# An attention and mixture-of-experts layer on one core: first sequence packed in quarters, slots cleared in pieces, first scatters at half pace, and later expert tiles two deep

## The chip, the cores and the metric

The kernel runs on one core of one Trainium2 chip. A core has TensorE (PE in the profile; its weight loads are listed as PEld), VectorE (DVE), ScalarE (ACT), GpSimd (POOL) and SyncE (SP). SP only issues transfers here. The metric is the device time in microseconds (us). The times shown are medians; one execution was also recorded by the hardware profiler.

## The reference

Eight sequences of 512 tokens with 128 features go through one layer: causal attention with 16 heads of 8 features, then a mixture of 8 experts of which each token uses two.

```python
# x: (8, 512, 128)
x = x + attn(layernorm(x))
#   s = (q * scale) @ k.T per head, causal mask, softmax, p @ v, then @ Wo + bo
x = x + ffn(layernorm(x))
#   probs = softmax(x_flat @ gate_w.T); topk_probs, topk_idx = top_k(probs, 2)
#   hidden = relu(einsum('th,ehf->tef', x_flat, w1) + b1)      # f = 512
#   all_out = einsum('tef,efh->teh', hidden, w2) + b2
#   y = sum over the two chosen experts of all_out * topk_probs
```

The kernel computes an expert only for the tokens that chose it.

## The kernel before

**Lanes.** The program is written by seven generators, called lanes here: `setup` (L175), `project` (L265), `shifts` (L355), `attend` (L450), `route` (L582) with `dispatch` (L675) inside it, `experts` (L756) and `sums` (L886). Each of them yields a due time, counted in sequences: 3.5 is halfway through the attention of sequence 3. The main loop at the end of the kernel always lets the lane with the smallest due time write its next instructions. The order in which instructions are written is the order on PE, ACT, DVE and SP. So the due times alone set what stands before what on each engine. POOL's indirect transfers are put in order with its masking instructions by `in_order` (L438).

**Attention.** `project` loads a sequence (L98), normalizes it, makes q and k, splits each into bf16 parts and writes the parts to DRAM (`to_dram`, L300). It reads them back packed by heads (L328) into `q2_buf[b % 2]` and `k2_buf[b % 2]`. For sequence 0 the q transfers go through SP's queue and the k transfers through ACT's; from sequence 1 on, all go through SP's. `shifts` computes the scores once (S, L393), takes the row maxima on DVE (L416), transposes them (`nmT`, L364) and writes them as two more rows into the packed q (L370). `attend` computes the scores again, transposed and with the maxima included (ST, L549), then the exponential on ACT (L555), the causal selection on POOL (L561) and the product with the values (L479). S runs 0.55 of a sequence ahead of ST.

**Experts.** The sequences form three groups: 0 to 3, 4 to 6, and 7. When the last sequence of a group is routed, `dispatch` gives each token two slots, sorted by expert in tiles of 128, and writes its rows there with indirect transfers (L734, two per 128 tokens; 32, 24 and 8 of them). The slots of a group, `xs`, were cleared before that by `setup` (L227), because a tile has empty places. The groups have 39, 31 and 15 tiles, 85 in all. `experts` works through them. Four tiles (a quad) are loaded at a time (`gather`, L807) and transposed on PE (L832, copied by ACT at L834). Per tile, SP loads the weights of the tile's expert (`wt`, 258 KB, L765), PE computes `ph` (L854, 8 instructions), ACT in even tiles (L862) or DVE in odd ones (L864) adds the bias and takes the relu into `hT`, PE computes `py` (L783, L788) one tile later, and DVE copies it into `yo` (L792). A quad is stored with one transfer (L797). `ph`, `py` and the transposes share three PSUM buffers (`ps_mm`); the attention scores have four (`ps_sc`).

**Sums.** `sums` fetches the two result rows of each token with indirect transfers (L917, one per 128 tokens and choice, 64 in all), and DVE multiplies them by their gate values and adds them to x (L899). Ten buffers hold the rows. A finished sequence is stored (L892).

The start and pace of each group's tiles are given by hand:

```python
    TILES_AT = ((5.56, 0.0705), (8.35, 0.03), (9.29, 0.03))
```

Of the kernel before, what the change touches and what calls it, by code (L numbers as in the profile page):

```python
# [18 lines left out]
P = 128  # L19
# [5 lines left out]
def preln_attn_moe(ctx: ExitStack, tc: tile.TileContext, x, wq, wk, wv, wo, bo,  # L25
# [149 lines left out]
    def setup():  # L175
# [34 lines left out]
        for l in range(3):  # L210
# [3 lines left out]
            if l < 2:  # L214
                rest = const.tile([E, D], F32, tag=f"b2r{l}", name=f"b2r{l}")
                V.tensor_tensor(rest, left, part, ALU.subtract)
                left = rest
        for e in range(E):
            yield 0.6 + 0.3 * e
            nc.sync.dma_start(out=wrows[e, :, 0:F], in_=w1[e])  # L220
            nc.sync.dma_start(
                out=w2_sb.rearrange("p (c e h) -> p c e h", c=FC, e=E)[:, :, e],
                in_=w2[e].rearrange("(c p) h -> p c h", p=P),
            )
        for k in range(len(GROUPS)):
            yield 3.1 + 0.3 * k
            nc.sync.dma_start(  # L227
                out=xs[k].rearrange("(c p) d -> p c d", p=P),
                in_=zeros.unsqueeze(1).to_broadcast([P, xs[k].shape[0] // P, D]),
            )  # L230
# [34 lines left out]
    def project():  # L265
        for b in range(B):
# [31 lines left out]
            def to_dram(s, dst, slots):  # L298
                for c, slot in slots:
                    queue[s].dma_start(  # L300
                        out=dst[slot].rearrange("d h t -> h d t"), in_=part[s][:, c, :]
# [11 lines left out]
            to_dram(0, q_parts, ((0, 0), (0, 3), (1, 1), (1, 4)))  # L313
            yield b - 1.18
            to_dram(0, q_parts, ((2, 2),))
            to_dram(1, k_parts, ((0, 0), (1, 1), (2, 2)))
# [6 lines left out]
            q2, k2 = q2_buf[b % 2], k2_buf[b % 2]  # L323
            for n in (slice(0, HG), slice(HG, H)) if b == 0 else (slice(0, H),):
                for s, dst, src in ((0, q2, q_parts), (1, k2, k_parts)):
                    for r in range(3):
                        o = r if src is q_parts else 0
                        queue[s].dma_start(  # L328
                            out=dst[24 * r : 24 * r + 24, n],
                            in_=src[o : o + 3, :, n].rearrange("c d h t -> (c d) h t"),  # L330
                        )
# [23 lines left out]
    def shifts():  # L355
# [11 lines left out]
        def rows(b, g, nmT):  # L367

            for l in range(2):
                nc.sync.dma_start(  # L370
# [304 lines left out]
    def dispatch(k, soon):  # L675
# [55 lines left out]
        for i in range(n * NT):  # L731
            yield soon(0.037 if group[-1] == B - 1 else 0.044)
# [23 lines left out]
    def experts():  # L756
        tiles = [(k, i) for k, g in enumerate(GROUPS) for i in range(tiles_of(len(g)))]
        wt, yo, at = {}, {}, {}

        def fetch(n):  # L760
            if n < len(tiles):
                k, i = tiles[n]
# [123 lines left out]
    def sums():  # L886
# [19 lines left out]
        t = 0  # L906
# [70 lines left out]
```

## Time and profile before

| | us |
|---|---|
| median of 9 runs | 784.3 (775.51 to 789.34) |
| profiled execution | 785.02 |
| its span | 783.3 |
| first scores (S) start | 31.24 |
| ST of sequence 0, 3, 5, 6 starts | 48.0, 216.5, 339.4, 417.4 |
| scatters of group 0 | 317.7 to 366.8 |
| first and eighth tile of group 0, ninth | 390.0, 425.4, 437.3 |
| attention ends | 568.0 |
| scatters of group 1 end | 584.1 |
| first tile of group 1, of group 2 | 601.0, 710.1 |
| last `py` ends | 765.2 |

The times of the profile count from the start of the span. Each row of a table of stretches gives a start and an end, the length, then the busy time of PE, PEld, DVE, ACT and POOL with the number of instructions in brackets, the mean clock that the throttle granted to TensorE as a share of full speed, the busy share of the DMA engines, and GB/s. In a row of the timeline stand the start, the duration, the engine, the line of the kernel, the operation and its tiles; in square brackets the time for which the engine was idle before it, and what ended that. "remote" is a release whose origin the profile doesn't tell. A row of waits gives the engine, operation and line that waited, what it waited for, the total in us, how often, and the longest.

### The profile page before, as it was taken

How to read it: one execution, taken by the hardware profiler on the slowest of the kernel's cores; microseconds unless marked ns; L12 is line 12 of the kernel's file. 1: busy time of each engine (PE TensorE's matmuls, PEld its weight loads, DVE VectorE, ACT ScalarE, POOL GpSimd, SP SyncE). 2: the span in 40 equal slices, each digit the busy share in tenths (PEclk: the TensorE clock that was granted, in tenths of full speed). 3: DMA queues.
4: the chain of work that ended last, by engine and by line, in shares of the span. 5: the costliest groups of instructions: out<-in, count | busy, mean ns of one | idle time of the engine just before them, and what ended most of it. 6: DMA issues, size and time to landing. Idle time of an engine off the chain costs nothing. (4 is left out here: it accounts for less than half of the span.)

```text
span 783.3 us, 13582 instructions
## 1 busy us (share of the span) xinstructions
PE 641.6 (82%) x4439; PEld 408.1 (52%) x4439; DVE 434.6 (55%) x1308; ACT 299.3 (38%) x651; POOL 272.2 (35%) x450
## 2 busy tenths in 40 slices
PE   5487898998996998887899799999958749787770
PEld 3233453454453454343467566776547738776660
DVE  3365768679676679534765475675114404341332
ACT  2043464564563563533465245454412112221110
POOL 4022233333332332786221112121760352422433
PEclk9677899898996997867899799998978869998885
DMA  3562164173277260252336422321532526664452
GB/s 91 132 150 41 29 162 110 29 176 96 55 190 232 55 130 7 81 140 77 82 96 147 125 60 80 89 78 39 151 90 68 166 68 170 186 175 135 130 149 64
DMA packets 78977, 84.81 MB, mean 108 GB/s; under 512 B 9852, under 2 KB 63660, under 8 KB 77756
## 3 DMA queue, kind: packets, MB, share of 16 engines
q1 hardware_dynamic: 74164, 73.97, 36.4%
q0 software_dynamic: 4096, 8.40, 3.8%
q10 hardware_dynamic: 648, 1.57, 0.8%
q8 instruction: 37, 0.61, 0.3%
q14 instruction: 32, 0.26, 0.1%
HBM read 57.74 MB, written 27.93 MB: 109 GB/s over the span
## 5 line engine op out<-in xcount | busy, mean ns | idle before, releaser
L416 DVE TENSOR_REDUCE pm<-s 128x1 f32<-128x512 f32 (+2 forms) x320 | 207.1, 684 | 118.7 <-PE s L403 111.4
L555 ACT ACTIVATE pt<-st 128x512 f32<-128x512 f32 x320 | 178.5, 598 | 131.2 <-PE st L549 113.1
L561 POOL TENSOR_SCALAR_AFFINE_SELECT pt<-pt 128x256 f32<-128x256 f32 x256 | 102.0, 412 | 304.5 <-ACT pt L555 302.4
L393 PE MATMUL s<-k,q 72*128 72x512 bf16 (+3 forms) x512 | 127.7, 330 | 16.9 <-DMA k<-ones_bf 12.3
L549 PE MATMUL st<-q,k 74*128 74x384 bf16 (+3 forms) x512 | 117.1, 330 | 13.5 <-DMA q<-nmT 4.4
L479 PE MATMUL po<-pt,va 128*9 128x512 f32 (+3 forms) x1024 | 114.2, 475 | 8.4 <-POOL pt L561 4.5
L854 PE MATMUL ph<-xgT,wt 128*128 128x128 f32 x680 | 103.3, 300 | 18.6 <-DMA wt<-wrows 5.7
L788 PE MATMUL py<-w_sb,hT 128*128 x680 | 108.3, 307 | 0.0
L854 PEld LDWEIGHTS ph<-xgT,wt 128*128 128x128 f32 x680 | 92.8, 212 | 27.0 <-issue 13.6
L788 PEld LDWEIGHTS py<-w_sb,hT 128*128 128x128 f32 x680 | 91.4, 209 | 14.7 <-issue 8.5
L917 POOL DMA_INDIRECT y<-ys,slot x64 | 60.7, 949 | 103.2 <-DMA ys<-yo 44.8
L862 ACT ACTIVATE hT<-ph,wt 128x128 f32<-128x128 f32 x172 | 49.3, 368 | 115.8 <-issue 58.0
L393 PEld LDWEIGHTS <-q 72*128 72x128 bf16 x512 | 50.1, 106 | 76.4 <-issue 49.3
L792 DVE COPY yo<-py 128x128 f32<-128x128 f32 x85 | 24.5, 289 | 115.0 <-PE py L788 65.4
L403 PE MATMUL s<-mask_bf,ident_bf 128*128 128x256 bf16 (+1 forms) x320 | 87.6, 274 | 0.0
L734 POOL DMA_INDIRECT xs<-xn_f,slot x64 | 62.3, 973 | 25.0 <-issue 15.7
L549 PEld LDWEIGHTS <-k 74*128 74x128 bf16 x512 | 47.7, 105 | 41.6 <-issue 21.5
L864 DVE TENSOR_SCALAR hT<-ph,wt 128x128 f32<-128x128 f32 x168 | 47.2, 343 | 32.7 <-PE ph L854 18.6
L479 PEld LDWEIGHTS po<-pt,va 128*9 128x9 f32 x1024 | 23.4, 90 | 69.7 <-issue 43.1
L403 PEld LDWEIGHTS <-ident_bf 128*128 128x128 bf16 x320 | 33.9, 106 | 3.7 <-issue 1.4
L834 ACT COPY xgT<-xgTp 128x512 f32<-128x512 f32 (+1 forms) x22 | 12.6, 572 | 55.5 <-PE xgTp L832 40.8
L832 PE MATMUL xgTp<-ident,xg 128*128 128x128 f32 x85 | 15.2, 306 | 19.6 <-DMA xg<-xs 17.6
(124 smaller groups left out, 520.6 us busy)
## 6 DMA issues: line engine op xcount, KB each, us to landing
wt<-wrows SPq DMA_DIRECT2D x85, 258.0 KB
q<-qparts SPq DMA_DIRECT2D x21, 384.0 KB
k<-kparts SPq DMA_DIRECT2D x21, 384.0 KB
qparts<-part SPq DMA_DIRECT2D x40, 128.0 KB
xg<-xs SPq DMA_DIRECT2D x19, 256.0 KB
ys<-yo SPq DMA_DIRECT2D x19, 256.0 KB
kparts<-part SPq DMA_DIRECT2D x21, 128.0 KB
xs<-zeros SPq DMA_DIRECT2D x1, 2496.0 KB
```

The lines of the kernel that those rows point to most:

```text
L393: nc.tensor.matmul(ps[:, at : at + (t + 1) * P], lhsT=q2[:KS, 2 * n + u, ts(t, P)], rhs=k2[:KS, 2 * n + u, : (t + 1) * P], start=(at == 0) ...
L403: nc.tensor.matmul(dst, lhsT=ident_bf, rhs=mask_bf if i > 0 else mask_bf[:, 0, :], start=False, stop=True, skip_group_check=True,)
L416: nc.vector.tensor_reduce(top, src, AX.X, ALU.max)
L479: nc.tensor.matmul(po[32 * h : 32 * h + VC, j * P :], lhsT=va[:, j, HG * g + h, :], rhs=at_cols(pts[pr], unit, u, at, W), start=(first and ...
L549: nc.tensor.matmul(ps[:, at : at + T - j * P], lhsT=k2[: KS + 2, 2 * n + u, ts(j, P)], rhs=q2[: KS + 2, 2 * n + u, j * P :], start=(at == ...
L555: nc.scalar.activation(pt[:, v, :], ps, AF.Exp, scale=SCALE)
L561: selects[0] = nc.gpsimd.affine_select(out=d, in_=d, pattern=[[0, 2], [1, P]], compare_op=ALU.is_ge, fill=0.0, base=0, channel_multiplier=-1,)
L734: ins = nc.gpsimd.indirect_dma_start(out=xs[k], out_offset=bass.IndirectOffsetOnAxis(ap=slot[k][:, j, i : i + 1], axis=0), in_=xn2[b0 + i ...
L788: nc.tensor.matmul(py, lhsT=hT[:, c, :], rhs=w2_sb[:, bass.ds(at[k, i] + c * E * D, D)], start=False, stop=(c == FC - 1),)
L854: nc.tensor.matmul(ph[:, ts(c, P)], lhsT=wt[k, i][:, ts(c, P)], rhs=xgT[:, ts(i - first, P)], start=True, stop=True,)
L862: nc.scalar.activation(hT[:, c, :], ph[:, ts(c, P)], AF.Relu, bias=bias)
L917: ins = nc.gpsimd.indirect_dma_start(out=y, out_offset=None, in_=ys[k], in_offset=bass.IndirectOffsetOnAxis(ap=slot[k][:, j, s * NT + c : ...
```

## The change

- `project`, sequence 0: the parts of q and k are written and read back in quarters of four heads, in the order write quarter 0, write quarter 1, pack quarter 0, write quarter 2, and so on. That makes 20 writes and 12 packs on SP's queue and 12 and 12 on ACT's. Before, 5 and 6 stood on SP's and 3 and 6 on ACT's.
- `shifts`, sequence 0: the rows of maxima are written through ACT's queue.
- `setup`: the loads of the expert weights and the clearing of the slots become 38 transfers of at most 256 KB, one every 0.085 of a sequence from 0.6 on. Before, the three clearings were one transfer each.
- `dispatch`: the scatters of group 0 have due times 0.09 apart instead of 0.044. As `dispatch` runs inside `route`, the routing of sequence 4 comes after them.
- `experts`, group 0: the tiles begin at 6.35 and are 0.05 apart, instead of 5.56 and 0.0705.
- `experts`, groups 1 and 2: `ph` lies in the score buffers (`ps_sc`), `hT` in the buffers of the exponentials, all `hT` and `yo` are made by ACT, `py` runs two tiles late, the weights lie in seven places of the packed q of even sequences and are fetched six tiles ahead, and the rows lie in eight places of the packed k and are loaded two quads ahead.
- `sums`: the fetched rows lie in five places of the packed q of odd sequences, a little less is left pending, and the last sequence is stored in two halves.

```diff
--- before.py
+++ after.py
+        pieces = []
         for e in range(E):
-            yield 0.6 + 0.3 * e
-            nc.sync.dma_start(out=wrows[e, :, 0:F], in_=w1[e])
-            nc.sync.dma_start(
-                out=w2_sb.rearrange("p (c e h) -> p c e h", c=FC, e=E)[:, :, e],
-                in_=w2[e].rearrange("(c p) h -> p c h", p=P),
-            )
+            pieces.append((wrows[e, :, 0:F], w1[e]))
+            pieces.append((
+                w2_sb.rearrange("p (c e h) -> p c e h", c=FC, e=E)[:, :, e],
+                w2[e].rearrange("(c p) h -> p c h", p=P),
+            ))
         for k in range(len(GROUPS)):
-            yield 3.1 + 0.3 * k
-            nc.sync.dma_start(
-                out=xs[k].rearrange("(c p) d -> p c d", p=P),
-                in_=zeros.unsqueeze(1).to_broadcast([P, xs[k].shape[0] // P, D]),
-            )
+            n = xs[k].shape[0] // P
+            for c in range(0, n, 4):
+                m = min(4, n - c)
+                pieces.append((
+                    xs[k].rearrange("(c p) d -> p c d", p=P)[:, c : c + m],
+                    zeros.unsqueeze(1).to_broadcast([P, m, D]),
+                ))
+        for n, (dst, src) in enumerate(pieces):
+            yield 0.6 + 0.085 * n
+            nc.sync.dma_start(out=dst, in_=src)
...
+            def to_dram(s, dst, slots, n=slice(0, H)):
                 for c, slot in slots:
                     queue[s].dma_start(
-                        out=dst[slot].rearrange("d h t -> h d t"), in_=part[s][:, c, :]
+                        out=dst[slot, :, n].rearrange("d h t -> h d t"),
+                        in_=part[s][HD * n.start : HD * n.stop, c, :],
+                    )
+            def pack(s, n):
+                dst, src = ((q2_buf, q_parts), (k2_buf, k_parts))[s]
+                for r in range(3):
+                    o = r if s == 0 else 0
+                    queue[s].dma_start(
+                        out=dst[b % 2][24 * r : 24 * r + 24, n],
+                        in_=src[o : o + 3, :, n].rearrange("c d h t -> (c d) h t"),
                     )
...
-            to_dram(0, q_parts, ((0, 0), (0, 3), (1, 1), (1, 4)))
-            yield b - 1.18
-            to_dram(0, q_parts, ((2, 2),))
-            to_dram(1, k_parts, ((0, 0), (1, 1), (2, 2)))
+            q_slots = ((0, 0), (0, 3), (1, 1), (1, 4), (2, 2))
+            k_slots = ((0, 0), (1, 1), (2, 2))
+            if b > 0:
+                to_dram(0, q_parts, q_slots[:4])
+                yield b - 1.18
+                to_dram(0, q_parts, q_slots[4:])
+                to_dram(1, k_parts, k_slots)
+            else:
+                quarters = [slice(HG * g, HG * g + HG) for g in range(G)]
+                for g in range(G + 1):
+                    if g < G:
+                        to_dram(0, q_parts, q_slots, quarters[g])
+                        to_dram(1, k_parts, k_slots, quarters[g])
+                    if g > 0:
+                        pack(0, quarters[g - 1])
+                        pack(1, quarters[g - 1])
+                yield b - 1.18
...
-            q2, k2 = q2_buf[b % 2], k2_buf[b % 2]
-            for n in (slice(0, HG), slice(HG, H)) if b == 0 else (slice(0, H),):
-                for s, dst, src in ((0, q2, q_parts), (1, k2, k_parts)):
-                    for r in range(3):
-                        o = r if src is q_parts else 0
-                        queue[s].dma_start(
-                            out=dst[24 * r : 24 * r + 24, n],
-                            in_=src[o : o + 3, :, n].rearrange("c d h t -> (c d) h t"),
-                        )
+            if b > 0:
+                pack(0, slice(0, H))
+                pack(1, slice(0, H))
...
-                nc.sync.dma_start(
+                (nc.scalar if b == 0 else nc.sync).dma_start(
...
-            yield soon(0.037 if group[-1] == B - 1 else 0.044)
+            yield soon((0.09, 0.044, 0.037)[k])
...
+        spare_q = q2_buf[0].rearrange("p h t -> p (h t)").bitcast(F32)
+        spare_k = k2_buf[0].rearrange("p h t -> p (h t)").bitcast(F32)
+        WTS, XGS = H * T // 2 // WROW, H * T // 2 // (4 * D)
+        fetched = [0, 0]
+        def ahead(k):
+            return 3 if k == 0 else WTS - 1
+        def behind(k):
+            return 1 if k == 0 else 2
+        def fetch_to(n):
+            while fetched[0] < min(n, len(tiles)):
...
+                if k == 0:
+                    wt[k, i] = work.tile(
+                        [P, WROW], F32, tag="wt", name=f"wt_{k}_{i}", bufs=4
+                    )
+                else:
+                    wt[k, i] = spare_q[:, ts(fetched[1] % WTS, WROW)]
+                    fetched[1] += 1
+                fetched[0] += 1
...
-            nc.vector.tensor_copy(yo[k, first][:, i - first, :], py)
+            if k == 0:
+                nc.vector.tensor_copy(yo[k, first][:, i - first, :], py)
+            else:
+                nc.scalar.copy(yo[k, first][:, i - first, :], py)
...
-            xg = work.tile([P, 4, D], F32, tag="xg", name=f"xg_{k}_{i}")
+            if k == 0:
+                t = work.tile([P, 4, D], F32, tag="xg", name=f"xg_{k}_{i}")
+            else:
+                q = len([a for a in xg if a[0] > 0]) % XGS
+                t = spare_k[:, ts(q, 4 * D)].rearrange("p (a d) -> p a d", a=4)
+            xg[k, i] = t
...
+                follow = quads[q + 1 : q + 2 + (k > 0)]
...
-            ph = mm_tile(f"ph_{k}_{i}")
+            if k == 0:
+                ph = mm_tile(f"ph_{k}_{i}")
+                hT = work.tile([P, FC, P], F32, tag="hT", name=f"hT_{k}_{i}")
+            else:
+                ph = ps_sc.tile([P, T], F32, tag="sc", name=f"ph_{k}_{i}")
+                hT = work.tile([P, 2, T], F32, tag="pt", name=f"hT_{k}_{i}", bufs=6)
+                hT = hT[:, 0, :].rearrange("p (c t) -> p c t", c=FC)
...
-                if n % 2 == 0:
+                if k > 0 or n % 2 == 0:
...
+            ready = late[: max(0, len(late) + 1 - behind(k))]
+            del late[: len(ready)]
+            for part in ready:
+                second(*part)
...
+            fetch_to(n + 1 + ahead(k))
+            if follow:
                 if i == first + (m - 2 if other else 0):
-                    xg = gather(*follow)
+                    for at_quad in follow:
+                        if at_quad not in xg and (other or at_quad[0] == k):
+                            gather(*at_quad)
+                            if other:
+                                break
...
+        YS = 5
+        got = [0]
...
+                _, b, c, n = done.pop(0)
                 nc.sync.dma_start(
-                    out=out[b].rearrange("(c p) d -> p c d", p=P), in_=xt[b]
+                    out=out[b].rearrange("(c p) d -> p c d", p=P)[:, c : c + n],
+                    in_=xt[b][:, c : c + n],
...
+                n = NT // 2 if b == B - 1 else NT
+                if (c + 1) % n == 0 and j == 1:
+                    done.append([0, b, c + 1 - n, n])
...
-                    add_up(4)
+                    add_up(3)
                     for j in range(2):
-                        y = work.tile([P, D], F32, tag="y", name=f"y_{b}_{c}_{j}", bufs=10)
+                        y = q2_buf[1].rearrange("p h t -> p (h t)").bitcast(F32)[:, ts(got[0] % YS, D)]
+                        got[0] += 1
...
-    TILES_AT = ((5.56, 0.0705), (8.35, 0.03), (9.29, 0.03))
+    TILES_AT = ((6.35, 0.05), (8.35, 0.03), (9.29, 0.03))
```

## The prediction

> **What bounds the kernel now.** I read the page's totals and its forty slices first, then the busy times by stretch, then single timelines. Three engine rows and the granted clock:
>
> ```profile
> PE 641.6 (82%) x4439; PEld 408.1 (52%) x4439; DVE 434.6 (55%) x1308; ACT 299.3 (38%) x651; POOL 272.2 (35%) x450
> PE   5487898998996998887899799999958749787770
> POOL 4022233333332332786221112121760352422433
> PEclk9677899898996997867899799998978869998885
> ```
>
> TensorE (PE) is the bound, but its holes (digits 4 to 7) stand in four places: the start, slices 13 and 14, slice 18, and everything from slice 29 on. The stretches:
>
> ```profile
> 240.00:260.00 20.00, 13.53 (x66) 6.53 (x67) 14.23 (x53) 6.87 (x14) 4.62 (x8) 0.66 0.52 159
> 340.00:360.00 20.00, 17.99 (x111) 8.57 (x110) 8.85 (x18) 8.66 (x16) 16.40 (x23) 0.76 0.70 175
> 417.00:568.00 151.00, 141.29 (x1130) 98.92 (x1128) 84.40 (x269) 70.81 (x163) 37.97 (x76) 0.94 0.37 98
> 601.00:762.00 161.00, 122.62 (x824) 109.06 (x825) 58.37 (x225) 32.42 (x104) 61.07 (x64) 0.86 0.51 143
> 620.00:640.00 20.00, 10.69 (x66) 9.54 (x64) 2.92 (x13) 1.95 (x6) 15.33 (x16) 0.80 0.46 129
> ```
>
> After start and length come PE, PE weight load, DVE, ACT, POOL, clock, DMA share and GB/s. While sequences 6 and 7 run with most of group 0's tiles PE works 141 of 151 us: full. From 601 on, with only tiles left, it works 123 of 161, and in 620-640 half the time although DVE and ACT are almost idle. The timeline there tells why:
>
> ```profile
> 628.82 1.06 PE L854 MATMUL ph<-xgT,wt 128*128 128x128 f32 x8
> 631.51 1.14 ACT L862 ACTIVATE hT<-ph,wt 128x128 f32<-128x128 f32 x4 [5.12 <-remote]
> 637.84 0.29 DVE L792 COPY yo<-py 128x128 f32<-128x128 f32 x1 [13.93 <-remote]
> 642.77 1.13 DVE L864 TENSOR_SCALAR hT<-ph,wt 128x128 f32<-128x128 f32 x4 [4.64 <-remote]
> ...
> 660.78 1.06 PE L854 MATMUL ph<-xgT,wt 128*128 128x128 f32 x8
> 661.93 1.14 ACT L862 ACTIVATE hT<-ph,wt 128x128 f32<-128x128 f32 x4 [0.36 <-PE ph L854]
> ```
>
> At 660.78 ACT starts 0.1 us after the matmuls end (661.84). Those of 628.82 end at 629.88, and DVE takes them up at 642.77. The trace's semaphore events put PE's completions in batches at 625.8, 631.4, 637.8 and 642.8, mean distance 5.7 us, just while POOL issues gathers back to back (620.1-640.3). Where POOL pauses, the delay is under 0.05 us. The cause I don't know; that the two go together I use.
>
> The other holes, SP's queue and the first matmul:
>
> ```profile
> 31.24 0.58 PE L393 MATMUL s<-k,q 72*128 72x512 bf16 x1 [12.25 <-DMA k<-ones_bf]
> 42.12 0.25 ACT L364 COPY nmT<-nmTp 32x128 bf16<-32x128 bf16 x1
> 45.49 1.21 SPq L370 DMA_DIRECT2D q<-nmT  x2
> ...
> 220.05 17.84 SPq L98 DMA_DIRECT2D x<-in_L_attn_x_dram  x1
> 237.99 1.29 SPq L370 DMA_DIRECT2D q<-nmT  x2
> ```
>
> The first scores wait 12.25 us for the packs. Row maxima ready at 42.4 are issued at 45.5, behind the q/k writes of sequence 1 (39.31-45.4). And a load stuck for 17.84 us behind the clearing of the slots holds the row maxima of sequence 3.
>
> **The change, part by part.** All terms are against the profiled execution: span 783.3, itself 785.0, 0.7 above the median of 784.3. A minus is a gain.
>
> *Start.* Before, 8 writes and 12 packs; the first q write goes at 12.31, the last at 19.74, and the first q packs, issued at 22.6, need 7.4 us because three 288 KB k packs are ahead of them. After: 32 writes of 32 KB and 24 packs of 96 KB, 32 of these issues on SP, 24 on ACT. At 0.35-0.6 us an issue, 32 take 11-19 us; SP's eleven of before, with their waits, end at 26.1. The first quarter's 8 writes take 4 us from 12.3, land after 2.3 (row: a 128 KB write) at 19, and its 96 KB packs land 2.5-2.9 us after issue when nothing is ahead (row: the first k packs), but stand behind quarter 1's writes. I get 24.5 if nothing collides, and the old 31.2 or later if everything queues; I take 29: -2. ACT holds 24 issues before va and the second sequence's xnT: at 0.4 us 10 us, to about 32, where va stood at 23; nothing needs va before ST at 48. With nmT on ACT, the 3.4 us from 42.1 to 45.5 go as well: ST could start at 43. But x_2 is issued at 51.8 and lands at 64.5 behind packs of sequence 1 (46.8-63.9), which the change leaves as they are, so most of the gain waits there. Net -1.5, ends +3 (ACT's or SP's issues late) and -7.
>
> The Trainium skill ("DMA: Bandwidth & Descriptors", section "Rules for kernel authors") speaks against this part: small transfers should be coalesced, below 64 KB one pays mostly overhead, and spreading over queues saves issue time only. Its fixed part, about 2.0 us a transfer, agrees with the 2.3 us of the 128 KB write; if 36 extra transfers paid it one after another, the start would be 72 us longer, but in the trace eight such writes, issued 12.3-19.7, are all down by 22.1, so they overlap.
>
> *Clearing in pieces.* 38 pieces of at most 256 KB, 0.085 apart, for 2.5, 2.0 and 1.0 MB at once. ST quarters of sequence 2 take 11.6, 14.9, 16.5, 11.3; of sequence 3, where the load blocks, 11.7, 20, 15.9, 11.2. The 5 us go; the same 5.4 MB cost 0-4 us in sequences 1 to 3, where the DMA share is lower. Take -4 (ends +3, -6).
>
> *Scatters at half pace.* 32 indirect DMAs at 1.27 us fill POOL in 317.7-366.8, and selects and so products wait behind them (POOL 16.4 of 20, clock 0.76). Sequence 4 takes 64.1 us where sequences 1 and 2 took 54; spread over twice the time: -7 (0, -10). Sequence 5 takes 78 with the rest of the scatters and 7 tiles; without tiles about 59: -19 (-13, -21). The tiles come back below. The stage of sequences 6 and 7 then begins at 417.4 - 31.5 = 386.
>
> *Group 0 from 6.35 at 0.05.* Sequences 6 and 7 take 150.6 us with 27 tiles, 12 us of it a stall (tile 7 at 425.4, tile 8 at 437.3: its weights wait behind sequence 7's packs of 417.8-421.6, which now fall before tile 6 or so; the stall could just as well move on). With 32 tiles: 150.6 - 12 + 5 x 2.32 = 150. The 2.32 is a dense tile: 660.78, 662.92, 665.06, 667.20 are 2.14 apart, plus a quarter of 0.63 for a quad's transposes. Attention ends at 536 instead of 568; the seven last tiles take 16, and group 1's scatters end, as before, 16 after attention: 552. From their end to the first tile of group 1 it is 16.9 us before (584.1 to 601.0), of which issue to landing of xg and to the matmul are 7 (594.04, 598.43, 601.00). Take 12: 564. On SP group 0's last store stands behind the row loads of group 1, which wait for these scatters, and the gathers wait for that store; the order was the same before.
>
> *Tail.* Before, 601.0 to 783.3 is 182 us for 46 tiles. New: ph has four score buffers, py runs two tiles late, weights come six ahead, rows two quads ahead, and hT and yo are ACT's: 1.14 + 0.29 + a quarter of 0.59 = 1.6 us a tile, under PE's 2.32. So DVE's adds no longer stand behind PE's reports, and POOL, which before lost 42.9 us to them,
>
> ```profile
> POOL y L917 <- DVE x L899: 42.9, 16, 12.7
> DVE yo L792 <- remote: 29.0, 5, 13.9
> ```
>
> gathers without pause: five places at 1.26 us are 6.3, above the 2.3-4.4 us of landing plus an add. That makes two long runs, 35 indirect DMAs (44 us) and 24 (30 us), just the condition of late reports. Dense bound: 46 x 2.32 = 107, plus the 18 us after the last py (765.2 to 783.3; the store in halves takes at most 1 off): 125. If each batch of 5.7 us lets only one tile through, as 625-646 did (four in 21), 13 are done in the runs: 74 + 33 x 2.32 + 18 = 169. Two tiles deep, two per batch is 26: 74 + 46 + 18 = 138. I take 1.5, the middle, as reports up to 9 us late leave the second buffer empty too: 153. DMA can carry it: a tile's 386 KB in 2.32 us are 166 GB/s, gathers add 52; 201 were measured in 680-700 at share 0.72.
>
> The skill's page "TensorE: Matmul & The Clock Gate" (Part 1) says that an idle window of some 3.4 us halves the clock; here 620-640 ran at 0.80 and 480-500, without a pause, at 1.00. If the clock fell to half in every batch, a tile's 2.14 us would double and one per batch would be all.
>
> *Sum.* 564 + 153 = 717 span, 719 execution, 718 on the median's scale.
>
> **The rivals.**
> - R1, two tiles hide the late reports altogether: 564 + 125 = 689, with a front a few us better or worse 672-702. For it: three ph's can be queued before PE needs an answer. Against: the yo copies need PE's report again, and three py buffers are shared with the transposes.
> - R2, the front gives little or the tail is as long as before: 564 + 182 = 746, 748 on the median's scale; with half of the 32 us lost as well, 764. For it: quad changes cost 3.3 us extra and the last landing governs them; scatter time moved from sequence 5 lies in 5 and 6 again.
> - R3, slower: the packed group 0. Its first tile is due at 6.40, 0.4 of a sequence of 75 us behind 386: 416. My 564 puts the 39 tiles 3.8 us apart; beyond 5.6 it is lost: 416 + 39 x 5.6 + 153 = 787. At the 6.9 us of 620-646 it is 838. For it: before, tiles 8 to 13 stood 5.8 apart (437.3 to 466.1), with PE full. Against: that was their due pace, 0.0705 of 75 us = 5.3; 0.05 gives 3.75.
> - The quarters don't do what they say (first s still at 31): 2 us, inside every case.
>
> **How the numbers follow.** About 0.5%, 4 us, is what a measurement can tell from no change. Forecast (700-740) 0.50, R1 0.14, R2 (740-780) 0.22, within 0.5% 0.03, R3 0.11. So faster 0.86, same 0.03, slower 0.11. The range 690-775 leaves out R3, no change and the outer ends of R1 and R2. The ends of the front's terms (-7 to -44 where the sum has -31.5) and of the tail (125 to 182) give 677 to 771; I move the low end up, since less needs every term at its best, and add a few us above for what the sum doesn't hold.
>
> **What would show it.** First s near 29, ST near 43-46, x_2's landing still near 60. No SP issue of 17 us near 220; quarter 2 of sequence 3 at 15 us. POOL under 0.6 busy where the scatters run; sequence 6 from about 386. Attention's end near 536; first tile of group 1 near 564; adds no more a releaser of gathers; two POOL stretches of 44 and 30 us at 1.26 a piece, with 3.5-4 us tiles inside and 2.3 us outside; last py near 698. I am wrong if reports stay late and the tiles run at 6 us in these stretches, if ACT's queue is the new wait (hT behind yo), if the weights land late (PE waiting on wt), or if sequences 6 and 7 stretch by more than the five tiles.

## The result, and the profile after

The changed kernel takes 797.1 us (median) where the kernel before takes 783.5 (the median of 62 runs beside it; 784.3 above is that of nine): a ratio of 1.019, with an interval of 1.017 to 1.021. It is slower. The prediction was 718, with a range of 690 to 775. The profiled execution shown here took 803.2 us (span 801.3), 6 us above the median; these 6 lie in sequence 6, at a lower clock (0.73 in 425-445 us, where most kernels that are the same up to there have 1.00).

| us | before | forecast | after |
|---|---|---|---|
| first scores | 31.2 | 29 | 31.3 |
| ST of sequence 6 starts | 417.4 | 386 | 382.2 |
| attention ends | 568.0 | 536 | 558.9 |
| scatters of group 1 end | 584.1 | 552 | 573.9 |
| first tile of group 1 | 601.0 | 564 | 595.2 |
| last `py` ends | 765.2 | 698 | 783.6 |
| span | 783.3 | 717 | 801.3 |

Attention's end is the end of the last ST matmul. Up to sequence 6 the forecast held within 4 us. The 84 us between forecast and span came later: 27 in the stage of sequences 6 and 7 (176.7 for 150), 8 from there to group 1 (36.3 for 28), and 53 in the tail (206.1 for 153), less the 4 gained.

The forty slices of the changed kernel's page, the same three rows as were shown of before:

```profile
PE   5496998998998989988499999999596119988191
POOL 4022233332332333867320111127407740004603
PEclk9659798897997997999686999899798559989586
```

Two new holes have a 1 in them: slices 32 and 33 (counted from 1), where POOL is at 7 and 4, and slice 38, where it is at 6. The stretches, with the columns that were explained above:

```profile
604.00:624.00 20.00, 10.52 (x57) 7.94 (x55) 6.29 (x27) 2.55 (x9) 15.33 (x16) 0.74 0.33 96
624.00:644.00 20.00, 3.22 (x9) 2.61 (x10) 4.27 (x12) 0.27 (x1) 15.20 (x16) 0.50 0.33 92
664.00:684.00 20.00, 20.00 (x160) 18.32 (x159) 0.00 (x0) 13.34 (x47) 0.00 (x0) 0.98 0.60 168
744.00:764.00 20.00, 4.75 (x17) 3.85 (x17) 4.56 (x13) 3.08 (x12) 10.59 (x12) 0.50 0.19 49
```

While POOL issues 16 indirect DMAs in 20 us (624-644), PE executes 9 matmuls. The gathers, and the last eight scatters among them, run from 602.4 to 652.8 and from 728.2 to 758 without a pause. At 659.5, 7 us after POOL has stopped, PE takes up its tiles again, and in 664-684 it works 20.00 of 20 us. Inside such a run the timeline shows PE, its weight loads and POOL:

```profile
634.29 0.94 POOL L988 DMA_INDIRECT q<-ys,slot  x1 [0.31 <-issue]
634.78 0.29 PEld L832 LDWEIGHTS py<-w_sb,hT 128*128 128x128 f32 x1 [2.51 <-issue]
635.54 0.94 POOL L988 DMA_INDIRECT q<-ys,slot  x1 [0.30 <-issue]
636.18 0.37 PE L832 MATMUL py<-w_sb,hT 128*128 x1 [2.43 <-issue]
636.79 0.94 POOL L988 DMA_INDIRECT q<-ys,slot  x1 [0.30 <-issue]
637.58 0.29 PEld L832 LDWEIGHTS py<-w_sb,hT 128*128 128x128 f32 x1 [2.51 <-issue]
638.04 0.95 POOL L988 DMA_INDIRECT q<-ys,slot  x1 [0.30 <-issue]
638.98 0.37 PE L832 MATMUL py<-w_sb,hT 128*128 x1 [2.43 <-issue]
```

Here one PE instruction starts every 1.40 us, a weight load and a matmul in turn, so a matmul every 2.80 us, where eight take 1.16 us together otherwise. The releaser is "issue": PE waits for no semaphore that the profile shows. This is more than the late completions that I had read in the trace of before. The waits from 595 us on say the rest:

```profile
POOL q L988 <- issue: 92.0, 55, 75.5
POOL q L988 <- DMA ys<-yo: 40.7, 2, 28.9
ACT yo L839 <- remote: 30.2, 3, 11.5
ACT hT L919 <- remote: 20.8, 1, 20.8
```

The wait of POOL for DVE's adds (42.9 us before) has left the list, as forecast; nothing paces the gathers any more. The other new hole, in slice 20, is at 385-399:

```profile
385.29 0.22 PE L427 MATMUL s<-mask_bf,ident_bf 128*128 128x128 bf16 x1
390.67 1.25 PE L262 MATMUL xnTp_f<-ident,xn_f 128*128 128x128 f32 x4 [5.17 <-DVE xn_f L255]
392.59 1.88 PE L622 MATMUL pl<-gwT,xnT_f 128*128 128x8 f32 x8 [0.68 <-ACT xnT_f L264]
398.58 0.21 PE L684 MATMUL pr<-sel,lower_bf 128*128 128x32 bf16 x1 [4.12 <-DVE before L674]
```

These are the steps of routing sequence 4, one behind the other, with no attention between them. The slow scatters keep the lane until 6.05; by then all due times of this routing (from 5.24) have passed, so the main loop writes them in one piece, and PE waits for most of these small steps on DVE.

### The profile page after: what moved, and what is told of

It is laid out like the page before. It is cut to its first block, busy times and chain, and to the rows that moved or that the text cites. A ratio compares the mean times of both kernels' runs of the same rounds, so it can differ in the third digit from the quotient of the medians.

```text
span 801.3 us, 13623 instructions
## 1 busy us (share of the span) xinstructions
PE 633.3 (79%) x4439; PEld 403.7 (50%) x4439; DVE 399.9 (50%) x1170; ACT 336.5 (42%) x789; POOL 271.7 (34%) x450
## 3 DMA queue, kind: packets, MB, share of 16 engines
q0 software_dynamic: 4096, 8.40, 3.7%
## 4 chain that ended last, share of the span: by engine, by line
PE 56%; DMA 10%; DVE 9%; issue 7%; another core or an unknown queue 6%; ACT 5%; POOL 4%; SPq 2%; ACTq 0%; POOLq 0%; DVEq 0%
PE py L832 12%; PE ph L912 11%; PE po L503 8%; PE st L573 6%; PE s L417 6%; DMA x<-in_L_attn_x_dram 4%; DVE pm L440 3%; DMA q<-qparts 2%; ACT pt L579 2%; PE s L427 2%; PE oqp L521 2%; PE pq L287 2%; PE xgTp L883 2%; PE py L827 2%
## 5 line engine op out<-in xcount | busy, mean ns | idle before, releaser
L417 PE MATMUL s<-k,q 72*128 72x512 bf16 (+3 forms) x512 | 124.8, 324 | 17.3 <-DMA qparts<-part 13.0
L503 PE MATMUL po<-pt,va 128*9 128x128 f32 (+3 forms) x1024 | 111.5, 470 | 5.0 <-POOL pt L585 4.7
L967 DVE SCALAR_TENSOR_TENSOR x<-q,gate,x 128x128 f32<-128x128 f32 x64 | 22.5, 352 | 168.3 <-DMA q<-ys,slot 165.7
L988 POOL DMA_INDIRECT q<-ys,slot x64 | 60.8, 950 | 134.8 <-issue 92.0
L912 PE MATMUL ph<-xgT,q 128*128 128x128 f32 x368 | 55.8, 293 | 35.0 <-issue 19.7
L919 ACT ACTIVATE hT<-ph,q 128x128 f32<-128x128 f32 x184 | 52.6, 371 | 66.9 <-remote 20.8
L912 PEld LDWEIGHTS ph<-xgT,q 128*128 128x128 f32 x368 | 50.7, 208 | 38.9 <-issue 21.8
L912 PE MATMUL ph<-xgT,wt 128*128 128x128 f32 x312 | 47.2, 299 | 0.2 <-ACT xgT L885 0.2
L912 PEld LDWEIGHTS ph<-xgT,wt 128*128 128x128 f32 x312 | 42.0, 209 | 4.0 <-issue 1.4
L919 ACT ACTIVATE hT<-ph,wt 128x128 f32<-128x128 f32 x80 | 22.9, 370 | 27.1 <-PE ph L912 15.0
```

The lines of the kernel that those rows point to most:

```text
L417: nc.tensor.matmul(ps[:, at : at + (t + 1) * P], lhsT=q2[:KS, 2 * n + u, ts(t, P)], rhs=k2[:KS, 2 * n + u, : (t + 1) * P], start=(at == 0) ...
L503: nc.tensor.matmul(po[32 * h : 32 * h + VC, j * P :], lhsT=va[:, j, HG * g + h, :], rhs=at_cols(pts[pr], unit, u, at, W), start=(first and ...
L912: nc.tensor.matmul(ph[:, ts(c, P)], lhsT=wt[k, i][:, ts(c, P)], rhs=xgT[:, ts(i - first, P)], start=True, stop=True,)
L919: nc.scalar.activation(hT[:, c, :], ph[:, ts(c, P)], AF.Relu, bias=bias)
L988: ins = nc.gpsimd.indirect_dma_start(out=y, out_offset=None, in_=ys[k], in_offset=bass.IndirectOffsetOnAxis(ap=slot[k][:, j, s * NT + c : ...
```

## The experiments

Theory 1: dense runs of POOL's indirect DMAs stop PE, and the change made them dense because DVE's adds no longer wait for PE. Theory 2: the two-deep arrangement with ACT as its engine costs the time. The miss in sequence 6 has a theory of its own, the late routing.

### Is it the gathers, and is it their bytes?

Two edits, each alone in the changed kernel: the gathers left out (the adds take a tile of zeros), and each gather replaced by a plain load that SP issues:

```diff
-                        y = q2_buf[1].rearrange("p h t -> p (h t)").bitcast(F32)[:, ts(got[0] % YS, D)]
+                        y = zeros
...
-                        ins = nc.gpsimd.indirect_dma_start(
...
-                        in_order(ins)
```

```diff
-                        ins = nc.gpsimd.indirect_dma_start(
...
-                        in_order(ins)
+                        r = ((s * NT + c) * 2 + j) * P
+                        nc.sync.dma_start(out=y, in_=ys[k][r : r + P])
```

> The changed kernel without the 64 gathers of result rows; DVE adds a tile of zeros in their place, so the mixture's sum is left out of the output. Theory 1: in the changed kernel PE stands almost still while POOL issues indirect DMAs back to back (608 to 652 and 735 to 757 us), and nothing else lengthens the tail. Then the tail from the first tile of group 1 (595 us) needs 46 x 2.32 + 15 = 122 us instead of 206, and the run takes 715 to 725 us. Theory 2: the two-deep arrangement itself (ACT with hT and yo, weights in seven places) is what costs; then the tail stays above 160 us and the run above 755.

> The changed kernel with each gather replaced by a plain load of 128 consecutive result rows, issued by SP: the same bytes arrive and the same adds run, but the rows are not those of the tokens. Theory 1 (POOL's back-to-back indirect DMAs hold PE): about as without gathers, 715 to 740 us; SP may lose some us, because a load that waits for a free place stands ahead of weight loads. If instead the traffic into SBUF or DVE's adds hold PE, it stays at 780 us or more.

Measured: 718.4 and 722.7 us, beside 787.3 for before. The tail falls to 127.5 us (588.9 to 716.4) and to 132 us. Theory 2 falls: two tiles deep on ACT, the tail is near the forecast's lower bound of 125 (though 5 us follow the last `py` here and not 18, as the last gathers are missing too). The bytes and the adds are not it either.

A third run lets POOL issue the plain DMA (`nc.gpsimd.dma_start`, same rows):

> The changed kernel with each gather replaced by a plain DMA of 128 consecutive result rows that POOL issues (the rows are not those of the tokens). If what holds PE is that POOL issues DMAs back to back, of whatever kind, it is as slow as the changed kernel: 780 to 800 us. If it is the work on 128 separate row addresses, it is like the loads from SP: 720 to 740 us.

711.0 us, beside 788.0. In 640-660 this kernel's row is

```profile
640.00:660.00 20.00, 20.00 (x163) 18.32 (x162) 7.25 (x22) 13.70 (x48) 10.62 (x20) 1.00 0.86 258
```

that is 20 POOL DMAs in 20 us, 258 GB/s, and PE full. The plain ones pass through the same queue of the profile as the indirect ones (q0, software_dynamic, 4096 packets in either kernel). So it is not that POOL issues DMAs, but that it issues indirect ones.

### Does the missing coupling make the run dense?

Forward, in the changed kernel:

```diff
-            if k == 0:
-                nc.vector.tensor_copy(yo[k, first][:, i - first, :], py)
-            else:
-                nc.scalar.copy(yo[k, first][:, i - first, :], py)
+            nc.vector.tensor_copy(yo[k, first][:, i - first, :], py)
```

> The changed kernel with the copy of py to yo back on DVE for all groups, and nothing else. Theory 1a: in the kernel before, the gathers were slowed by DVE, whose adds stood behind copies that waited for PE; that coupling kept the runs of gathers short, and the change removed it. Then gathers get gaps again, the tail is 150 to 175 us and the run takes 740 to 770. Theory 2 (ACT as the new bound): DVE's help is worth at most the 0.29 us of a copy, under 14 us in 46 tiles, and PE still stands in long runs of gathers: 783 to 797.

And backward, in the kernel before, which keeps its buffers and its order one tile deep:

```diff
-                if n % 2 == 0:
+                if k > 0 or n % 2 == 0:
...
-            nc.vector.tensor_copy(yo[k, first][:, i - first, :], py)
+            if k == 0:
+                nc.vector.tensor_copy(yo[k, first][:, i - first, :], py)
+            else:
+                nc.scalar.copy(yo[k, first][:, i - first, :], py)
```

> The kernel before with one thing of the change: for groups 1 and 2 all relu steps (hT) and all copies yo are made by ACT, so that DVE's adds stand behind nothing that waits for PE. Depth, buffers and the ten places for gathered rows stay as before. Theory 1a (the coupling of gathers to PE through DVE kept the runs of indirect DMAs short): the gathers now run without gaps, PE stands still for most of 30 to 45 us after group 0's store and 25 us after group 1's, and the time is 800 to 850 us. Theory 1b (the stall needs the change's buffers or its two-deep order): no such stall, 775 to 790 us.

The one copy back on DVE: 739.3 us, 0.940 of before (0.933 to 0.947). POOL waits for DVE again, and PE keeps working. Its waits and its stretch:

```profile
DVE yo L836 <- PE py L832: 66.5, 27, 8.1
POOL q L985 <- DVE x L964: 31.7, 14, 3.6
```

```profile
640.00:660.00 20.00, 18.27 (x138) 16.67 (x138) 4.84 (x18) 10.82 (x38) 9.59 (x11) 0.95 0.77 213
```

The kernel before with free adds (`hT` has moved to ACT here as well): 825.8 us beside 788.0, single runs, and the standstill is there without the change's buffers, places or depth:

```profile
640.00:660.00 20.00, 2.26 (x9) 1.78 (x8) 5.53 (x16) 0.17 (x1) 15.12 (x17) 0.50 0.21 53
760.00:780.00 20.00, 2.07 (x8) 1.88 (x9) 4.93 (x14) 0.90 (x4) 11.35 (x13) 0.50 0.17 43
```

It has another form here. The eight matmuls of a step still come together, but their completion is reported ever later: two of its waits from 601 us on are

```profile
ACT yo L795 <- remote: 40.5, 3, 22.1
PE ph L857 <- issue: 31.8, 2, 20.1
```

The longest belongs to a `py` that ends at 642.5 and that ACT takes up at 662.3.

Both directions agree: a copy that waits for PE, ahead of the adds on DVE, is a brake on the gathers. In the kernel before it doesn't space them; it ends a dense run early: POOL's timeline of 620-653 has the same 16 indirect DMAs in the same order as with free adds, with gaps of 0.30 us, and then the brake:

```profile
620.10 1.00 POOL L734 DMA_INDIRECT xs<-xn_f,slot  x1 [8.53 <-DVE mine L708]
...
639.35 0.94 POOL L917 DMA_INDIRECT y<-ys,slot  x1 [0.30 <-issue]
653.03 0.94 POOL L917 DMA_INDIRECT y<-ys,slot  x1 [12.74 <-DVE x L899]
```

With free adds this run goes on to 668.9, and PE stands still from 642.5 to 662.6.

### How large a pause is enough?

A memset on POOL after each gather, in three sizes (here 512), and a kernel with two places for gathered rows:

```diff
                         in_order(ins)
+                        pause = work.tile([P, 512], F32, tag="pause", name=f"pause_{b}_{c}_{j}", bufs=1)
+                        in_order(nc.gpsimd.memset(pause, 0.0))
```

> The changed kernel with a memset of 128 x 1024 on POOL after every gather, about 1 to 1.5 us each, so that gathers come some 2.3 to 2.8 us apart instead of 1.25. Theory 1: a pause between two indirect DMAs is enough to let PE's work through; tail 125 to 160 us, run 720 to 755. If any work of POOL holds PE, or if the number of gathers counts and not their density, the run is at 797 or longer, since the runs of POOL become twice as long.

> The changed kernel with a memset of 128 x 512 on POOL after each gather: about 0.5 us, where 128 x 1024 took 0.97 us and PE ran dense (20.00 of 20 us in 640 to 660). Gathers come about 1.6 us apart. If the pause needed is as short as that, 725 to 745 us, since the gathers of the tail are through sooner than with the long pause (754 us); if PE is still held in part, 755 to 790.

> The changed kernel with a memset of 128 x 256 on POOL after each gather: about 0.3 us, gathers some 1.4 us apart, between the 1.25 that stop PE and the 1.65 that don't. 735 to 750 if 1.4 is enough; 760 to 797 if it isn't (where the chip stalls at all).

> The changed kernel with two places for gathered rows in place of five, so that each gather waits for the add of the one before the last: landing 2.3 us and an add give one gather per 1.7 to 2.5 us, with POOL idle in between instead of busy. If idleness serves as well as a memset, PE runs dense and the time is 735 to 765 us.

| memset | its time, us | gather to gather | PE busy of 20 us in a run | time, us |
|---|---|---|---|---|
| none | - | 1.25 | 3.22 | 797 |
| 256 | 0.33 | 1.45 | 12.67, 11.24 | 779.2 |
| 512 | 0.54 | 1.65 | 20.00 | 738.1 |
| 1024 | 0.97 | 2.08 | 20.00 | 754.4, ratio 0.962 (0.955 to 0.969) |

The three stand on three chips, with before at 789.9, 788.0 and 787.3; 256 and 512 are single runs.

With the memset of 512 the timeline reads:

```profile
643.18 0.54 POOL L996 MEMSET pause<- 128x512 f32 x1
643.55 1.16 PE L832 MATMUL py<-w_sb,hT 128*128 x8
643.89 0.95 POOL L988 DMA_INDIRECT q<-ys,slot  x1 [0.17 <-issue]
644.83 0.55 POOL L996 MEMSET pause<- 128x512 f32 x1
644.98 1.06 PE L912 MATMUL ph<-xgT,q 128*128 128x128 f32 x8
```

POOL is as busy as ever; only its indirect DMAs are 0.4 us further apart, and PE is dense. At 1.45 us PE's matmuls still come singly or in twos and threes, most of these starts 0.7 to 1.5 us apart. So the limit lies between 1.45 and 1.65 us in these runs. The long pause costs at the end: the last `py` ends at 709.4, and the gathers go on until 748. The kernel with two places overwrites a place before its add has read it, so its output isn't the sum. Its gathers came in pairs some 5 us apart, and PE was dense beside them (tiles 2.1 us apart from 625 on, last `py` 723.4), but the gathers themselves took until 773: 780.9 us.

### The late routing

```diff
+        now = [0.0]
         for b in range(B):
-            now = [b + 1.24]
+            now[0] = max(now[0], b + 1.24)
```

> The changed kernel with one due time mended: the routing of sequence 4, which the slow scatters push from 5.24 to 6.05, gets its steps 0.035 apart from there on, where the change has them all overdue, so that they are written in one piece with nothing between them. In the changed kernel PE stands 13 us in that piece (385 to 399 us) and runs at clock 0.5 to 0.6 until 410. Theory: the stage of sequences 6 and 7 (ST of 6 to the end of attention: 167 to 170 us in the runs so far, where 150 was forecast) loses 8 to 14 us, attention ends at 538 to 546 instead of 549 to 555; the total falls by as much. Rival: the waits move to other places and attention ends at 549 to 555 as before.

Attention ended at 536.3 us, where the twelve runs with the change's late routing have 549 to 560. In 380-400 PE is busy 19.09 of 20 us (9.56 in the changed kernel). The whole run took 689.4 us beside 759.6, far less than expected: on this chip PE did not stand still, with gathers 1.25 us apart. That was so in all four kernels that ran there; here the one with undone quarters:

```profile
620.00:640.00 20.00, 20.00 (x162) 18.32 (x161) 6.24 (x18) 13.86 (x49) 14.20 (x15) 1.00 0.80 232
...
624.06 1.16 PE L820 MATMUL py<-w_sb,hT 128*128 x8
625.05 1.06 PE L900 MATMUL ph<-xgT,q 128*128 128x128 f32 x8
625.23 0.95 POOL L976 DMA_INDIRECT q<-ys,slot  x1 [0.31 <-DMA q<-ys,slot]
626.20 1.16 PE L820 MATMUL py<-w_sb,hT 128*128 x8
626.48 0.94 POOL L976 DMA_INDIRECT q<-ys,slot  x1 [0.30 <-issue]
```

Is it the chip? The unaltered changed kernel and the paced routing, on two further chips:

> The changed kernel itself, unaltered, beside the two below. On the chip of the last four runs gathers 1.25 us apart did not hold PE (20.00 of 20 us), and before took 760 us there; on the two chips of the runs ahead of them they did, and before took 784 to 788. If the stall belongs to the chip, this run shows before near 785 with the changed kernel near 797 and two standstills of PE of 25 to 45 us, or before near 760 with the changed kernel near 710 and none. If it comes and goes on one chip, the times of the rounds scatter between the two.

> The kernel with the paced routing a second time, unaltered. It took 689 us on the one chip where before took 760. If before is near 785 here and PE stands still while the gathers run 1.25 us apart, the stall belongs to the chip and not to the variant: 797 less 14, about 783. If it takes 689 to 700 beside a before of 785, the variant is what avoids the stall.

The changed kernel again took 798.6 us beside 789.6 (ratio 1.011, 1.006 to 1.016), with both standstills. The paced routing took 781.9 beside 789.9, with a standstill (no tile between 594.0 and 636.6), and attention ended at 536.5. So the stall goes with the chip, and the gain of the pacing (13 us or more to attention's end) with the kernel. All runs on one chip were made close together, so a passing condition of that chip isn't told from the chip itself. Of the five chips of these experiments the standstill was seen on three (before at 788 to 790), on a fourth with before at 787 no kernel with free gathers ran, and on the fifth (before at 760) it was absent.

The kept traces settle what the totals leave open. Their semaphore events tell when each completion of PE was reported. Of some 1150 in each of the four traces of the fifth chip none comes over 1 us after its matmul's end. In each of the sixteen other traces 21 to 93 do, every one within 8 us of an indirect DMA of POOL: on the fourth chip too, where the first experiments ran, and in the kernel before (52). And from the end of group 1's scatters to its first tile it takes 7.5 to 8.0 us on the fifth chip, and 17 to 23 us on the others, except in the last kernel below, which pauses after its scatters. Free of the stall, the three variants of the next section, each the changed kernel with one part undone, take 0.93 to 0.94 of before; the forecast's 718 is 0.92.

### The other parts, each undone alone

> The changed kernel with the scatters of group 0 back at 0.044, so that the routing of sequence 4 isn't late either. Prediction's step: half pace is worth 7 us in sequence 4 and some in sequence 5, so sequence 4 takes 62 to 66 us instead of 56.5. Rival: the piece without gaps (13 us in sequence 6) costs more than the half pace gains, and attention ends earlier than 549.

> The changed kernel with the expert weights and the clearing as before (whole slots in one transfer at 3.1, 3.4 and 3.7). Prediction's step: the clearing in pieces is worth 4 us, all of it in sequence 3: ST of sequence 3 to ST of sequence 4 takes 58 to 59 us instead of 54.3, and sequences 1 and 2 take 0 to 2 less each. Rival: other transfers fill the gain, and from ST 1 to ST 4 the three sequences take 163 to 164 us either way.

> The changed kernel with sequence 0 packed as before, in halves, with the rows of maxima on SP again. Prediction's step was -1.5 us; the changed kernel showed first scores at 31.3 to 33.4 us and ST 0 at 46.2 to 49.5, against 31.2 and 48.0 before, so the expectation now is that nothing is lost by undoing it: first scores 31 to 32, ST 1 at 108 to 112. Rival: the quarters do gain, but the transfers in pieces take it away again; then ST 1 comes 2 us or more later than the 109.7 to 112.6 seen with quarters.

These three ran on the chip without the stall: 712.9, 709.2 and 711.6 us beside 759.6. I read their stages, since the totals are single runs.
- Scatters at 0.044: sequence 4 takes 64.0 us (56.5 to 57.6 with the slow ones on that chip), sequence 5 takes 67.5 (50 to 55). In exchange there is no late routing, the stage of sequences 6 and 7 takes 153, and attention ends at 559.4. With the half pace, late routing and all, it ends at 556 to 557 on that chip. By these single runs the rival is out, but only just: the half pace gains some 23 us up to sequence 6 and loses most of them again.
- Clearing whole: sequence 3 takes 58.4 us where pieces gave 54.1 to 54.6, sequences 1 to 3 together 165.6 for 163.8 to 164.8 on that chip, and ST of sequence 6 starts at 391.1 for 382 to 383. The pieces are worth 1 to 2 us there and 2 to 5 in sequences 4 and 5.
- Halves instead of quarters: first scores at 31.2, ST 1 at 108.2. Four kernels with halves have ST 1 at 107.4 to 112.4, fourteen with quarters at 109.2 to 113.2. The quarters do nothing that can be seen. (The Trainium skill, "DMA: Bandwidth & Descriptors", section "Rules for kernel authors", warns of transfers below 64 KB; here 32 writes of 32 KB for 8 of 128 KB, and 24 packs for 12, cost no measurable time, so what each of them costs beyond its bytes mostly overlaps.)

### What both repairs give

Paced routing and halves, with the memset of 512 after the gathers of groups 0 and 1, or with `yo` on DVE; then the memset after the scatters of groups 1 and 2 as well:

> The changed kernel with the routing of sequence 4 paced, sequence 0 packed in halves as before, and a memset of 128 x 512 on POOL after each gather of groups 0 and 1. Sum from the runs: 738 with the short pause, less 14 (attention's end 536 for 549 to 555), less 2 of the start, less 3 without pauses at the end: 719 on a chip where the changed kernel stalls; where it doesn't, 685 to 700.

> The changed kernel with the routing of sequence 4 paced, sequence 0 packed in halves as before, and yo copied by DVE. Sum: 739 less 14 less 2: 723 where the changed kernel stalls; where it doesn't, 680 to 695.

> The best kernel so far (725 us beside a before of 790) with the pause after the scatters of groups 1 and 2 as well. Its trace shows PE's completions 5 to 8 us late at 535 to 552, where 11 scatters follow one another. If they come in time with pauses, group 1 starts 0 to 6 us earlier although the scatters take 4 us longer: 716 to 726. If the scatters are the longer chain, 728 to 732.

725.3 us (0.921 of before, 0.916 to 0.927), 729.4 (0.926, 0.921 to 0.932), and 716.6 (0.908, 0.904 to 0.911). The sum of the single gains held within 7 us. With pauses after the scatters too, the run of tiles is full:

```profile
540.00:560.00 20.00, 17.77 (x141) 15.27 (x142) 7.08 (x26) 5.68 (x16) 18.16 (x26) 1.00 0.40 114
580.00:600.00 20.00, 20.00 (x163) 18.33 (x162) 6.44 (x25) 13.70 (x47) 17.27 (x23) 1.00 0.75 218
600.00:620.00 20.00, 20.00 (x162) 18.32 (x162) 1.94 (x6) 13.63 (x48) 18.00 (x25) 1.00 0.77 216
620.00:640.00 20.00, 20.00 (x162) 18.32 (x162) 4.51 (x13) 13.74 (x48) 18.01 (x25) 1.00 0.65 182
```

From attention's end to the first tile of group 1 it takes 28.2 us (542.5 to 570.7), and 35.2 without the pauses after scatters (534.4 to 569.6), although the scatters themselves take longer. Group 1 begins no earlier for it, since attention ends 8 us later in this execution, 5 of them there already at sequence 6; the gain lies behind, with 118 us for 122 from group 1's first tile to the last `py`.

## Why the prediction was wrong, point by point

- **Tail, the step that failed.** "If each batch of 5.7 us lets only one tile through ... 13 are done in the runs" was to be the worst case, "I take 1.5, the middle": 20 tiles in 74 us. Measured were 8 in 80: three begin in the first 5 us of the first run and one more, at 615.4, until 659.5; the second run has three and one as well. The rate came from 620-646 of before. POOL issued its indirect DMAs there as densely as in the changed kernel (eight scatters and eight gathers in 20 us, where I read gathers only), but DVE's adds ended that run after 20 us. I named this coupling, forecast its end, and priced runs of 44 and 30 us by a run that it had cut off. In a longer one the delay grows: reports 2 to 4 us late in that row of before became 20 us with free adds, and the changed kernel's PE fell to a matmul per 2.8 us. How it depends on the length alone, no run varies. The bound "tail unchanged" (182) had the same fault. (Four starts in 21 us are also 6.9 us a tile, as R3 says, and not 5.7; that is worth 5 us.)
- **What remains right of it:** without this stall the two-deep tail takes 129 to 130 us with all its gathers (forecast's bound 125), gathers run 1.25 us apart, and the two runs of 44 and 30 us were 50 and 30.
- **The clock.** I had weighed the Trainium skill's rule that idle windows halve the clock ("TensorE: Matmul & The Clock Gate", Part 1) as an aside. The trace agrees: 0.50 at 624-664. It is a consequence here: at half the clock a tile's eight matmuls take 2.08 us for 1.06 (659.50), which is little beside one tile in 50 us.
- **Sequences 6 and 7 at 150 us.** Paced, they take 154 to 156 (382.4 to 536.3; 380.9 to 536.5): the term was nearly right. It left out that dispatch sits inside the routing lane, so that slow scatters make the next routing late and bunch it: 13 us. I had said in the change's description that the routing comes after the scatters, and priced nothing for it. Eight kernels that are the same up to there take 167 to 170 us; the 176.7 of the table hold the 6 us named above too.
- **Up to sequence 6:** 382.2 for 386. Sequences 4 and 5, with terms of -7 and -19, gave -7.5 and -25.6; part of the surplus may be routing that now runs in sequence 6, which no run tells apart. The pieces were about right, the quarters worth nothing where -1.5 stood. I had the first q write at 12.3 us and eight writes before the first packs; in the trace SP's first one goes at 16.73, ten stand before its first pack (25.46), and the first scores start at 31.28.
- **From attention to group 1:** 36 for 28 us. The scatters ended 15 us after attention (16 forecast), and from there to the first tile it was 21.3 us where 12 were taken. Late completions beside the scatters (`hT` and `oT` waiting 6.5 and 10.8 us on "remote") fit this: with pauses between the scatters these 21 us become 7.8.
- **The rivals.** Slower, R3, came true in sign by another mechanism: group 0's tiles stood 4.4 us apart (422.3 to 589.3), below the 5.6 that it needed. A tail near R1's 125 us came only without gathers, with plain loads, or on the chip without late reports, so R1's reason (two tiles hide them) didn't hold. No rival priced gathers that stop PE for a whole run.

## What to carry to other kernels

Before decoupling two engines, ask what the wait between them was holding back: a wait that looks like loss can be the brake that keeps a harmful rate down, and a rate read from a run that the brake cut short doesn't bound the longer run that follows. GpSimd's indirect DMAs beside TensorE work are better spaced (1.65 us apart was enough here, 1.45 not) than issued as fast as they go, and it is worth trying on more than one chip. Where lanes with due times share one generator, a delay in the first part makes the next part's due times lapse, and its steps lose the other work that used to fill their gaps.

## What the runs showed of the hardware

- With indirect DMAs of 128 rows of 512 bytes 1.25 us apart (0.95 of issue and a gap of 0.30), the changed kernel's matmuls stop coming together some 7 us after the start of such a run (602.4 to 609.4; 728.2 to 735.3): most come singly, 0.7 to 2 us apart, and later 2 to 3.5 us. In the kernel before with free adds they stay together, but their completion is reported up to 20 us late. At 1.45 us apart PE works 11 to 13 of 20 us; at 1.65 it works 20.00, though some completions still come 2 us late. Plain DMAs of POOL, 0.54 us each, do no harm at 20 in 20 us. Beside the dense scatters of group 1 (561-574 us) PE's matmuls came together, but completions were taken up to 7 us late (`oTp` ends at 569.2, ACT copies it at 575.9).
- Why, no run tells. It is not the traffic (258 GB/s did no harm), not the packets of POOL's queue (1166 in 618-650 with plain DMAs, 703 in 625-653 with the stall), not a semaphore wait of PE in the profile, and not POOL being busy. Nor does the trace show a fetch of instructions as the wait: the instruction queues moved three packets in 602-653, in 2.0, 0.43 and 0.32 us. What POOL and PE share there stays open.
- One chip of the four on which free gathers ran didn't show it. There the kernel before took 760 us instead of 788 to 790, so that the same effect seems to cost the kernel before some 25 us elsewhere. Its 52 late reports fit this; no trace of it on that chip was kept to show it.
